# Hints for the branch at the end of a decoder kernel, and another order of tokens in its last sums

## The chip, the cores and the metric

The kernel runs on one core of a Trainium2 chip. The metric is the device time of one execution in microseconds. Three runs of the kernel before took 683.02, 683.12 and 683.7 us; the median is 683.12.

## The reference

The reference is a decoder of two layers for 4 sequences of 256 tokens, width 256, with a layer norm after each of its six blocks. Each layer has a self-attention, a cross-attention to a context of 1,601 rows and a feed-forward block. What matters here is the last block, a mixture of eight experts of which each token takes two, and the layer norm behind it:

```python
logits = SOFTCAP * jnp.tanh((x @ w_gate) / SOFTCAP)
probs = jax.nn.softmax(logits, axis=-1)
_, idx = jax.lax.top_k(probs, TOPK)                      # two of eight experts
weights = probs * jax.nn.one_hot(idx, E).sum(-2)
for e in range(E):
    h = jax.nn.silu(x @ w1[e]) * (x @ w3[e])
    out = out + h @ w2[e] * weights[:, e:e + 1]
x = _layernorm(x + out, axis=-1)
```

## The kernel before, in words

Five engines run queues of instructions, each in order: TensorE (PE), VectorE (DVE), ScalarE (ACT), GpSimd (POOL) and SyncE (SP), which issues most transfers. The program doesn't write these queues by hand. Every operation is entered into a list with its inputs, outputs and a planned cost, and `weave` (L319) then places them one by one. It takes the operation that can start first (key at L344: planned start, then priority) and appends it to its engine's queue. An operation can start when its inputs' planned ends, with a latency between the engines, have come and its engine is free. A VectorE operation of n elements is planned to be ready after `us` and to free its engine a little earlier (L244 and L245), an operation with no engine (`None`) starts at the latest planned end of what it depends on:

```python
us = 0.155 + n * (0.00055 if method == "tensor_scalar" and chip else 0.00105)
...
return us - 0.085, us
```

The planned times only fix the order. On the chip, semaphores decide when an instruction starts.

The experts' work is done in tiles of 128 rows. A tile holds tokens of one expert. `route` writes each token's row twice into a list in DRAM (`lists`), with the gate's weight and a number, its slot, behind the 256 values. The slots come from `places` (L1263 to L1266). `expert_tile` (L1439) reads 128 rows of a list (xg), multiplies them with w1 and w3 of the tile's expert (pa, in two banks of PSUM), makes h out of them (ScalarE's tanh, then two VectorE operations; tile name eh), multiplies h with w2, and makes y (tile name ey) on VectorE. VectorE then makes the row numbers (tile name slots, two small operations, L1509 to L1514), and GpSimd scatters y into rows of a DRAM tensor `yd` (L1515, issued at L1293). Each token has two rows in yd, one for each of its experts.

As many tiles as are surely needed are 20; three more exist (RARE) for an unlucky split of the tokens. The last two of the 20 tiles (`last`) don't scatter: they make a matrix `pick` of zeros and ones out of their slots (L1503 to L1508), and `add_up` (L1517) multiplies y with it, so that TensorE adds each row to its token's place in PSUM (`acc`, one bank for each of the four batches of 256 tokens). I count tiles from 1: tile 18 is the last that scatters, tiles 19 and 20 are added up. TensorE does the first products of tiles 18 and 19 one behind the other, then the w2 product of 18, the first products of tile 20, the w2 products of 19 and 20, and then the sums into acc.

SyncE reads yd back with eight transfers (L1693), two for each batch (tile name entry), which wait for all scatters. Partition p gets rows 2p and 2p+1 of its batch, which lie beside each other.

What follows stands in a branch with two arms (`end`, L1571; the switch at L1588). A number `enough` is 1 when the three rare tiles aren't needed. `ask` (L1562) lets each of the five engines read it into a register, once pick of tile 19 has been made. At the switch each engine jumps for itself into arm 0, which does the rare tiles and then `leave`, or arm 1, which does `leave` alone. Here arm 1 is taken. At an arm's start each engine runs a BRANCH_PREFETCH_HINT for the branch at the arm's end, which the switch puts there by itself.

`leave` (L1522) finishes the layer norm. GpSimd adds the two halves that were read from yd (L1541), four sums in a row. VectorE adds acc of batch b, then makes the mean and variance of batch b - 1 (L1543 to L1551), GpSimd makes rstd out of the variance in two operations (L1553, L1554), and `go` (L1526) makes nmr on VectorE, lets ScalarE scale the batch (for the last batch VectorE does one half) and issues the output's transfer. In VectorE's queue the order is: sum of batch 0, sum 1, statistics 0, sum 2, statistics 1, nmr 0, sum 3, statistics 2, nmr 1, statistics 3, nmr 2, nmr 3. In GpSimd's queue the four sums come first and the rstd pairs behind them.

Of the kernel, the functions around the change:

## Time and profile before

One execution was profiled. Its time was 681.36 us, its span from the first to the last instruction 679.6 us.

| what | value |
|---|---|
| profiled execution, us | 681.36 |
| its span, us | 679.6 |
| median of three runs, us | 683.12 |
| PE busy, us (share) | 650.4 (96%) |
| DVE busy, us (share) | 445.1 (65%) |
| ACT busy, us (share) | 305.9 (45%) |
| POOL busy, us (share) | 126.3 (19%) |
| granted TensorE clock | 0.993 |
| transfers | 85.37 MB, mean 126 GB/s |
| last TensorE sum ends, us | 668.0 |
| last output transfer issued, us | 675.34 |

PE, DVE, ACT, POOL and SP are the five engines; a q behind the name (DVEq) is the engine's sequencer, which runs branches, register and semaphore instructions. All matrix products stand at L271 and all other operations at L408, since two helpers issue them; they are told apart by the names of their tiles. In a timeline each line has the start and the length in us, engine, line, operation, tiles (out<-in) and, in brackets, how long the engine was idle before it and what released it. In the chain of waits each line is a stretch of the path that ended last. The semaphores' times and the packets of the transfers, with those of the instruction queues that bring the engines' code, are in the trace beside it.

### The profile page before, as it was taken

How to read it: one execution, taken by the hardware profiler on the slowest of the kernel's cores; microseconds unless marked ns; L12 is line 12 of the kernel's file. 1: busy time of each engine (PE TensorE's matmuls, PEld its weight loads, DVE VectorE, ACT ScalarE, POOL GpSimd, SP SyncE). 2: the span in 40 equal slices, each digit the busy share in tenths (PEclk: the TensorE clock that was granted, in tenths of full speed). 3: DMA queues.
4: the chain of work that ended last, by engine and by line, in shares of the span. 5: the costliest groups of instructions: out<-in, count | busy, mean ns of one | idle time of the engine just before them, and what ended most of it. 6: DMA issues, size and time to landing. Idle time of an engine off the chain costs nothing.

```text
span 679.6 us, 12351 instructions
## 1 busy us (share of the span) xinstructions
PE 650.4 (96%) x4373; PEld 517.3 (76%) x4373; DVE 445.1 (65%) x1196; ACT 305.9 (45%) x948; POOL 126.3 (19%) x169
## 2 busy tenths in 40 slices
PE   9999999999999999999989999999999899999993
PEld 6778788668877677786767767777866689999992
DVE  6899887433525844456499997867778665545433
ACT  4779766211132333334346786746645522222212
POOL 3331132122300000000022001131211321211114
PEclk9999999999999999999999999999999899999998
DMA  9932121536999614000020060000020282897423
GB/s 305 351 120 64 36 75 41 160 91 233 319 302 342 215 62 132 0 1 1 0 56 1 23 227 1 1 24 9 17 87 1 85 305 101 271 341 248 158 87 132
DMA packets 61456, 85.37 MB, mean 126 GB/s; under 512 B 4478, under 2 KB 43780, under 8 KB 61380
## 3 DMA queue, kind: packets, MB, share of 16 engines
q1 hardware_dynamic: 59604, 79.83, 36.2%
q0 software_dynamic: 1632, 4.48, 1.8%
q8 instruction: 39, 0.64, 0.4%
q14 instruction: 37, 0.30, 0.1%
q10 hardware_dynamic: 144, 0.13, 0.1%
HBM read 67.29 MB, written 17.13 MB: 124 GB/s over the span
## 4 chain that ended last, share of the span: by engine, by line
PE 79%; DVE 13%; ACT 4%; issue 2%; POOL 1%; DVEq 0%; POOLq 0%; ACTq 0%
PE bank L271 70%; PE bank L278 9%; ACT at L408 3%; DVE at L408 3%; DVE nm L408 2%; DVE x L408 1%; DVE as L408 1%; DVE h L408 1%; DVE st L408 1%; POOL rstd L408 1%; DVE entry L408 1%; DVE fm L408 0%; DVE hq L408 0%; DVE kf L408 0%; ACT fm L408 0%
## 5 line engine op out<-in xcount | busy, mean ns | idle before, releaser
L408 ACT ACTIVATE at<-at,nm 128x128 f32<-128x128 f32 (+1 forms) x256 | 106.3, 419 | 23.4 <-DVE nm L408 22.6
L271 PEld LDWEIGHTS bank<-xgT,wt 128*128 128x128 f32 x640 | 73.3, 192 | 1.5 <-ACT xgT L408 1.0
L271 PE MATMUL bank<-xgT,wt 128*128 128x128 f32 x640 | 73.9, 275 | 0.5 <-ACT xgT L408 0.5
L278 PE MATMUL bank<-ident,at 128*128 128x128 f32 (+1 forms) x440 | 61.6, 277 | 2.0 <-DVE at L408 1.8
L278 PEld LDWEIGHTS bank<-ident,at 128*128 128x128 f32 (+1 forms) x440 | 50.6, 142 | 14.3 <-issue 6.6
L271 PE MATMUL bank<-V,aT 128*128 128x256 f32 (+1 forms) x240 | 55.1, 380 | 0.6 <-DVE o L408 0.6
L271 PE MATMUL bank<-KT,qT 128*128 128x512 f32 (+1 forms) x128 | 54.7, 554 | 0.0
L271 PEld LDWEIGHTS bank<-V,aT 128*128 128x128 f32 (+1 forms) x240 | 45.2, 190 | 10.6 <-issue 3.6
L271 PE MATMUL bank<-kf,V 128*128 128x256 f32 (+1 forms) x208 | 50.0, 382 | 1.1 <-DVE kf L408 1.1
L408 POOL TENSOR_SCALAR rstd<-mv 128x2 f32<-128x2 f32 (+1 forms) x26 | 5.8, 223 | 242.9 <-DVE mv L408 179.2
L408 DVE TENSOR_REDUCE nm<-at 128x4 f32<-128x512 f32 (+1 forms) x64 | 50.6, 807 | 0.4
L271 PE MATMUL bank<-wkv,KT 128*128 128x256 f32 (+1 forms) x208 | 49.6, 382 | 0.0
L408 ACT ACTIVATION_READ_ACCUMULATOR at<-at,nm 128x1 f32 x256 | 48.5, 189 | 0.0
L271 PEld LDWEIGHTS bank<-kf,V 128*128 128x128 f32 (+1 forms) x208 | 38.5, 190 | 7.3 <-DVE kf L408 2.3
L271 PEld LDWEIGHTS bank<-wkv,KT 128*128 128x128 f32 (+1 forms) x208 | 37.9, 186 | 7.0 <-issue 1.0
L408 ACT COPY aT<-bank 128x512 f32<-128x512 f32 (+2 forms) x58 | 30.7, 554 | 26.5 <-PE bank L278 25.8
L408 DVE TENSOR_REDUCE m<-bank 128x1 f32<-128x512 f32 (+1 forms) x32 | 20.4, 639 | 29.7 <-PE bank L271 29.7
L408 POOL TENSOR_TENSOR at<-at,rs 128x512 f32<-128x512 f32 (+1 forms) x20 | 22.9, 1143 | 87.6 <-DVE rs L408 80.4
L408 DVE TENSOR_TENSOR at<-at,rs 128x512 f32<-128x512 f32 (+1 forms) x44 | 38.4, 872 | 0.9
L408 ACT ACTIVATE fm<-bank 128x512 f32<-128x512 f32 (+2 forms) x33 | 17.9, 551 | 45.6 <-PE bank L271 45.0
L271 PE MATMUL bank<-w2e,eh 128*128 x160 | 37.7, 380 | 0.0
L408 DVE TENSOR_TENSOR at<-bank,cmask 128x256 f32<-128x256 f32 (+1 forms) x64 | 33.2, 545 | 5.3 <-PE bank L271 5.1
(267 smaller groups left out, 1230.0 us busy)
## 6 DMA issues: line engine op xcount, KB each, us to landing
wt<-in_w SPq DMA_DIRECT2D x40, 512.0 KB, 5.2
lists<-h SPq DMA_DIRECT2D x6, 1548.0 KB, 19.2
KT<-in_ctxT SPq DMA_DIRECT2D x6, 1024.0 KB, 6.1
V<-in_ctx SPq DMA_DIRECT2D x6, 1024.0 KB, 6.4
w2e<-in_w SPq DMA_DIRECT2D x8, 512.0 KB, 7.5
KT<-in_ctxT SPq DMA_DIRECT2D x6, 577.0 KB, 6.0
V<-in_ctx SPq DMA_DIRECT2D x6, 512.0 KB, 4.2
xg<-lists SPq DMA_DIRECT2D x20, 129.0 KB, 4.1
```

Of the source, the lines that this page charges most:

```text
L271: lambda: self.nc.tensor.matmul(real(o), real(lhsT), real(rhs), start=real(start), stop=stop, **kw)
L278: fns.append(lambda: self.nc.tensor.transpose(real(o), real(x), real(ident)))
L408: return getattr(engine, method)(*[real(x) for x in args], **{k: real(x) for k, x in kw.items()})
```

## The change

`ask` becomes `tell`, which is called twice. It reads `enough` into a register on the engines that it is given, then gives these engines a hint for the switch (`tc.switch_hint`), which computes the address of the arm that will be taken and hands it to the engine's instruction prefetch. VectorE, GpSimd, SyncE and ScalarE read and hint when h of tile 19 is planned to be done; TensorE when y of tile 19 is. `expert_tile` returns h as well for that.

The slots in `places` are no longer 2p + t for the token of partition p and half t but p + 128 t, so a token's row in yd is the token's own number. Reading yd back is unchanged and now gives partition p the tokens 2p and 2p + 1, and the output is written in that order: 2 KB in a row from each partition for batches 0 to 2. `iotaT` and so `pick` are unchanged.

```diff
         places = pool.tile((P, B, 2, 2), F32, "places")
         k.gpsimd.iota(
-            places, [[S, B], [1, 2], [T, 2]], base=1, channel_multiplier=2, allow_small_or_imprecise_dtypes=True
+            places, [[S, B], [P, 2], [T, 2]], base=1, channel_multiplier=1, allow_small_or_imprecise_dtypes=True
         )
...
-            return pick, y
+            return pick, y, h
...
-    def add_up(b, into, pick, y, first=False):
+    def add_up(b, into, pick, y, _, first=False):
...
-            to = out[b * S : (b + 1) * S, :].rearrange("(t p) d -> p t d", p=P)
+            to = out[b * S : (b + 1) * S, :].rearrange("(p t) d -> p t d", p=P)
...
-    def ask(enough, picked):
-
-        engines = (nc.tensor, nc.vector, nc.gpsimd, nc.sync, nc.scalar)
+    def tell(enough, what, *engines):
 
         def emit():
-            where.update({e.engine: e.value_load(enough.real()[0:1, 0:1], min_val=0, max_val=1) for e in engines})
-
-        k.op({None: (0.0, 0.1, emit)}, [], [enough, picked], unordered=True)
+            mine = {e.engine: e.value_load(enough.real()[0:1, 0:1], min_val=0, max_val=1) for e in engines}
+            tc.switch_hint(mine, 2, "end")
+            where.update(mine)
+
+        k.op({None: (0.0, 0.1, emit)}, [], [enough, what], unordered=True)
...
-            for arm in tc.Switch(where, 2):
+            for arm in tc.Switch(where, 2, "end"):
...
         if last == 0:
-            ask(enough, two[0])
+            tell(enough, two[2], nc.vector, nc.gpsimd, nc.sync, nc.scalar)
+            tell(enough, two[1], nc.tensor)
```

## The prediction, made before the result

> **What bounds the kernel now.** I first read the page's row of busy engines: PE is busy for 96% of the span, so only the last stretch, where PE has nothing left, can be shortened by this change. Then the chain of waits from 655 us on. Its columns are start, length, work.

> ```profile
> 654.96 6.15 PE bank L271 x40
> ...
> 661.38 0.06 DVEq L1769
> 661.44 5.55 issue
> 667.00 0.06 DVEq L1588
> ...
> 667.20 0.06 DVE entry L408
> ...
> 670.83 0.04 DVE nmr L408
> 670.87 0.60 DVE entry L408
> ...
> 673.49 0.17 DVE nmr L408
> ```

> VectorE's branch (L1769) ends at 661.44, and the first instruction of its arm, the hint at L1588, starts 5.55 us later. "issue" means that no recorded work explains it. The packet records of the instruction queue do: two 8 KB packets start at 665.04, one for VectorE and one for SyncE, 3.6 us after VectorE's branch, because the reads of yd hold the 16 DMA engines from 658.85 to 665.65. GpSimd and ScalarE branched before those reads and needed only 2.6 and 2.4 us. So the arm's code arrives late, and the additions (entry) begin at 667.20.

> Next, what else those additions need: the timeline of GpSimd, and SyncE's waits.

> ```profile
> 655.12 0.96 POOL L1293 DMA_INDIRECT yd<-ey,slots  x1 [7.91 <-DVE slots L408]
> 661.78 1.27 POOL L408 TENSOR_TENSOR entry<-entry 128x512 f32<-128x512 f32 x1 [5.69 <-DMA entry<-yd]
> 663.58 3.99 POOL L408 TENSOR_TENSOR entry<-entry 128x512 f32<-128x512 f32 x3 [0.54 <-DMA entry<-yd]
> 669.45 0.23 POOL L408 TENSOR_SCALAR rstd<-mv 128x2 f32<-128x2 f32 x1 [1.89 <-DVE mv L408]
> 669.77 0.72 POOL L408 TENSOR_TENSOR rstd<-rstd,mhalf 128x2 f32<-128x2 f32 x1
> ```

> ```profile
> SPq L285 <- DMA yd<-ey,slots: 20.1, 1, 20.1
> ```

> The last scatter goes out at 655.12, lands at 657.71 (its semaphore), and only then does SyncE issue the eight reads of yd. GpSimd's four sums of what they bring end at 667.57, and its rstd work comes behind them. This second chain is covered by 5.55 us of missing code today.

> Last, the group of L1567, the reading of `enough`, as VectorE pays for it now (min/median/max ns, first and last start):

> ```profile
> L1567 DVEq EVENT_SEMAPHORE  x5: 49/50/50, 616.8 to 617.2; - x5
> ...
> L1567 DVEq TENSOR_LOAD <-enough x1: 543/543/543, 617.7 to 617.7; - x1
> L1567 DVEq FUSED_REGOPS  x1: 222/222/222, 618.3 to 618.3; - x1
> L1567 DVEq SEQ_ASSERT  x1: 31/31/31, 618.5 to 618.5; - x1
> ```

> From the first of these at 616.82 to the next vector operation at 618.61 VectorE's queue stands still for 1.79 us. The five waits are for events long past, since this is the first time that VectorE's sequencer reads; they go wherever the read goes.

> **The change, part by part.**

> *The hint itself (a gain at VectorE).* What does a hinted branch cost? Each arm starts with a hint for the branch at its end: VectorE's second branch, at 674.49, is 75 ns long and the next instruction starts at 675.07, behind a 0.41 us operation; SyncE's ends at 676.07, next 676.47. So 0.4 us, against 5.55. PE gives the counter-example: hint at 667.62, branch at 668.34, and that branch lasts 4.18 us, so a hint needs some 2.5 us (what GpSimd and ScalarE waited for a load with idle DMA). VectorE's new hint should come at about 656.0, its branch at 661.4: 5 us. [...] by the rows it starts its arm at 661.8. I take the rows. [...]

> *Where the read and hint land.* The planner, from which I take an order and no time, gives `tell` the end of h of tile 19 as its start. It counts VectorE free 0.085 us before a result ends (L245), so ey of tile 18, which is ready by then, is placed first, and slots of tile 18, which needs ey, after. VectorE's queue becomes: eh of 19, ey of 18, **read and hint**, slots of 18, eh of 20. Behind the read stand the two slots operations, and for them waits the last scatter; for it the eight reads of yd; for those GpSimd's four sums.

> *Its price there.* ey of 18 runs from 654.10 to 654.59; today slots follows at 654.50. In the trace the next operation came 1.05 us after the end of the operation ahead of the read (617.56 to 618.61). The hint adds two MOVE, a FUSED_REGOPS and the hint: 0.24 us from the rows ahead of VectorE's branch (661.14 to 661.38) and 0.11 for the hint with its gap (667.00 to 667.10). So slots starts at 654.59 + 1.05 + 0.35 = 655.99, **1.5 us later**. Bounds: 0.9 if the read need not wait for the operation before it and the old waits vanish; 2.0 if the read is slower or an assertion is added. The row is exact for this read, so 1.5. eh of 20 (656.51) is still untouched by it.

> *What that does downstream.* Scatter 656.62, landing 659.21, reads from 659.26. The DMA engines are saturated by them (2 MB in 6.8 us), so everything shifts: GpSimd's last sum ends at 667.57 + 1.50 = 669.07. Only then rstd of batch 0: 0.06 gap, 0.31 to the start of pow (669.45 to 669.77), 0.73 to its event (669.77 to 670.50), so 670.18, and nmr of batch 0 on VectorE at 670.24 instead of 670.74. VectorE itself is no longer late: its additions wait for GpSimd's sums at 664.5, 666.4, 667.8 and it has the statistics of batch 1 done by 669.5. But the addition of batch 3 stands behind nmr of batch 0 on VectorE's queue, so it starts at 670.29 instead of 670.79. PE's sums end at 668.01 and are not last. From that addition on the order and lengths are those of today: **0.50 us gained** to the end. In general the gain is 2.0 minus the delay of slots: with no delay nmr would start at 668.74.

> *The other engines' reads and hints: nothing.* ScalarE: between the activation at 650.59 and own at 654.67, some 4 us for about 1.6; without the cover eh of 20 would slip. GpSimd: between scatters that end at 647.2 and start at 655.12. SyncE: before its 20 us wait, ahead of the eight reads, all done long before they may go. TensorE: after the second products of tile 20 and before the sums into acc. Its read took 0.70 (617.07 to 617.77), hint 0.38: 1.08. The sequencer has issued tile 20's last products by about 658.85, and the sums' first operand (ey of 19) is announced at 659.90, their first weight load starts at 660.71: hidden, at worst 0.3, and 1.1 without that cover. What is taken away at 579 (GpSimd) to 618 was hidden under PE, which had no gap there: no gain. Earlier arms on GpSimd, ScalarE and SyncE gain nothing either: they then wait for data (661.78, 670.96, 672.07).

> *The order of tokens.* The iota of places has as many elements. Scatters still write 1 KB rows. The last outputs of batches 0 to 2 go out as 128 pieces of 2 KB instead of 256 of 1 KB: a 1 KB packet took 48 ns in the outputs, a 2 KB packet 94 ns in the reads of yd, so 0.77 and 0.75 us on 16 engines: nothing. Batch 3's halves keep 1 KB pieces, with a stride of 2 KB in DRAM, which no row here shows; bounds 0.3 either way for the tail, value 0.

> *Sum.* Profiled execution 681.36 (span 679.6 and 1.76 around it) minus 0.50 is 680.86. The median of the runs is 1.76 above that execution; carried over, 683.12 - 0.5 = **682.6**.

> **Rivals.**
> - *The read costs VectorE little* (faster). If slots were delayed by no more than 0.6 us, the gain is 1.4 or more; with no delay 683.12 - 2.0 = 681.1. For it: VectorE idles 1.04 us just ahead of ey of 18, where a read would be nearly free. Against: the planned order puts it behind ey. 18%.
> - *The hint doesn't carry to VectorE's branch* (slower; place: 661.44). Its block is not kept or never fetched. Then the fetch queues behind the reads of yd as before, and these now end 1.5 us later: the packet starts at 666.5, the arm at 668.5, and everything after it 1.5 us later than today: 684.6. It decides as soon as the block is missing at 661.44 while the reads run. [...] Against: the packets of the instruction queue (25 of 8 KB from 22 to 655 us for 3,118 recorded instructions of four engines) make a line about 125 instructions, of which VectorE runs 12 between hint and branch, and its last crossing fits the 0.4 us gap at 617.3, 70 instructions before. 14%.
> - *The likeliest*, one wait replaced by another, 0.1 to 1.1 us gained: 682.0 to 683.0. 68%.

> **How the numbers follow.** A measurement of this kernel tells 0.2% (1.4 us) from no change. So faster 0.18, same 0.68, slower 0.14 are the three cases. The range reaches from the faster rival's 681.1 to 684.2, which leaves out the worst of the slower one and the tails, together under 2 in 10; the likeliest alone has 682.0 to 683.0.

> **What would show it.** Right: no "issue" of microseconds behind VectorE's branch; slots of 18 near 656.0 and the last scatter near 656.6; GpSimd's sums ending near 669.1 and nmr of batch 0 waiting for rstd near 670.2; PE's sums ending at 668.0 as before. Wrong: slots still at 654.5 (then about 681.1); a gap of more than 1 us between VectorE's branch and its arm (then about 684.6); or a gap on PE ahead of the sums at 660.9.

## The result, and the profile after

The kernel after takes 683.68 us (median of 20 runs), the kernel before in the same comparison 682.25 (20 runs): a ratio of 1.0023, 95% interval 1.0012 to 1.0033. It is slower by 1.4 us, where I had forecast 0.5 us less. The profiled execution of after took 684.53 us, its span is 682.8.

The two profiled executions differ by 3.2 us, twice what the medians do. TensorE's last sum ends at 670.23 us instead of 668.00, and up to there nearly every instruction of the experts' stage comes 2.2 us later. Of this 1.91 us is there when VectorE makes `enough` (581.36 us instead of 579.45), ahead of everything that hints and reads can touch: it is the spread of executions, in which the last sum lies between 666.40 and 670.36 over all 16 profiled kernels of this study. The other 0.32 us comes behind it. From `enough` to the last sum it is 88.87 us in the kernel after, 88.84 in e4 and 88.54 or 88.55 in all others, e6 below among them, which reads the number at the same places. So below I count from TensorE's last sum wherever two kernels are compared.

These are lines of the kernel after for reading the number (L1565), the hint (L1566), the branch (L1770) and the beginning of an arm (L1588), those of VectorE and SyncE. The columns are engine and operation, number, min/median/max ns, first and last start. The first start of L1770's COMPARE_BRANCH is the branch in question, the second is the one at the arm's end:

```profile
L1565 DVEq TENSOR_LOAD <-enough x1: 542/542/542, 656.8 to 656.8; - x1
...
L1566 DVEq BRANCH_PREFETCH_HINT  x1: 68/68/68, 658.2 to 658.2; - x1
...
L1770 SPq COMPARE_BRANCH  x2: 37/52/67, 666.5 to 679.5; - x2
...
L1770 DVEq COMPARE_BRANCH  x2: 63/73/83, 663.6 to 678.0; - x2
...
L1588 SPq BRANCH_PREFETCH_HINT  x1: 36/36/36, 667.0 to 667.0; - x1
...
L1588 DVEq BRANCH_PREFETCH_HINT  x1: 45/45/45, 669.3 to 669.3; - x1
```

VectorE is given its hint at 658.2, branches at 663.6 and starts its arm at 669.3: 5.65 us, as long as without a hint (5.55). Its instruction packet starts only at 666.77, 3.2 us behind the branch. SyncE, hinted at 584.1, needs 0.46 us from branch to arm instead of 4.98. Of the other engines (not shown) TensorE profits (0.4 us instead of 3.3), ScalarE (2.8 instead of 2.4) and GpSimd (2.65 and 2.63) don't.

GpSimd's timeline of the kernel after:

```profile
658.92 0.96 POOL L1292 DMA_INDIRECT yd<-ey,slots  x1 [9.48 <-DVE slots L408]
665.02 1.26 POOL L408 TENSOR_TENSOR entry<-entry 128x512 f32<-128x512 f32 x1 [5.13 <-DMA entry<-yd]
667.70 1.27 POOL L408 TENSOR_TENSOR entry<-entry 128x512 f32<-128x512 f32 x1 [1.42 <-DMA entry<-yd]
670.24 1.27 POOL L408 TENSOR_TENSOR entry<-entry 128x512 f32<-128x512 f32 x1 [1.28 <-DMA entry<-yd]
671.87 1.27 POOL L408 TENSOR_TENSOR entry<-entry 128x512 f32<-128x512 f32 x1 [0.36 <-DMA entry<-yd]
673.11 0.23 POOL L408 TENSOR_SCALAR rstd<-mv 128x2 f32<-128x2 f32 x1
```

Less the 2.23 us by which TensorE is late in this execution, the scatter goes out 1.57 us later than before, but the last sum starts 3.34 us later: now the third and fourth sum wait for their reads too, and the last three have 0.4 to 1.4 us of idle time ahead. And rstd follows at once, where in the kernel before GpSimd had 1.89 us to spare ahead of it. The chain of waits has turned accordingly (start, length, work):

```profile
658.92 2.55 DMA yd<-ey,slots
...
664.50 1.24 SPq L285
...
665.79 5.92 DMA entry<-yd
...
671.87 1.27 POOL entry L408
673.14 0.21 POOL rstd L408
673.35 0.07 issue
673.42 0.74 POOL rstd L408
674.16 0.02 issue
674.18 0.16 DVE nmr L408
```

VectorE's missing code, which ended last before, is no longer on it, though it is still missing. The path is scatter, reads of yd, GpSimd's sums, rstd, nmr.

One stretch of this chain is new: SyncE's seventh issue, at 664.50, takes 1.24 us, where the others take 0.34 to 0.57. SyncE's eight issues of before, of after and of e6 (below), in this order:

```profile
657.76 3.74 SPq L285 DMA_DIRECT2D entry<-yd  x8
661.53 4.68 SPq L285 DMA_DIRECT2D entry<-yd  x8
658.74 3.67 SPq L285 DMA_DIRECT2D entry<-yd  x8
```

So in the kernel after the last read goes out 0.94 us later behind the first than before. TensorE's hinted packet is under way for most of that issue (664.41 to 665.37 us). In the other kernels seven of SyncE's issues take over 0.1 us more than usual, and six of these have an instruction packet beside them; that the packet holds them up is not shown.

**A rule for the end.** nmr of batch 0 comes at the later of two times: 3.55 us after VectorE's first addition (its own queue: 667.20 to 670.74 before), or 1.04 us after the end of GpSimd's last sum (673.14 to 674.18 after). From it to the last nmr it is 3.7 to 3.8 us in every kernel. In all 16 profiles the rule gives nmr of batch 0 within 0.05 us. (The fourteen kernels e1 to e14 are the experiments below.) The table has these times, counted from the end of TensorE's last sum. "Reads" is the time from the first of SyncE's eight issues to the end of the last 2 KB packet. "PE packet" says whether a 16 KB packet of TensorE's instruction queue starts within the first 7 us of them. In the eight kernels without one a packet of TensorE, fetched behind its branch, still starts 7.1 to 8.2 us behind the first issue, ahead of the end of the reads. A dash stands where VectorE's path ends before TensorE's last sum.

| kernel | VectorE branch to arm, us | reads, us | PE packet | VectorE's path | GpSimd's path | nmr 0 | ratio to before, interval |
|---|---|---|---|---|---|---|---|
| before | 5.55 | 7.89 | no | 2.75 | 0.61 | 2.74 | 1 |
| after | 5.65 | 9.42 | yes | 2.84 | 3.95 | 3.95 | 1.0023 (1.0012 to 1.0033) |
| e1 hints earlier | 0.52 | 9.64 | yes | - | 2.14 | 2.14 | 0.9984 (0.9975 to 0.9994) |
| e2 behind a crossing | 5.85 | 9.11 | yes | 3.04 | 1.81 | 3.04 | 1.0001 (0.9989 to 1.0012) |
| e3 order alone | 4.57 | 7.90 | no | 1.76 | 0.82 | 1.76 | 0.9993 (0.9981 to 1.0004) |
| e4 after slots | 5.44 | 9.46 | yes | 2.65 | 1.69 | 2.65 | 0.9995 (0.9982 to 1.0007) |
| e5 = e1, no PE hint | 0.52 | 9.00 | no | - | 1.54 | 1.54 | 0.9981 (0.9969 to 0.9993) |
| e6 = after, no PE hint | 4.80 | 7.94 | no | 1.98 | 2.44 | 2.44 | 1.0007 (0.9996 to 1.0017) |
| e7 = e2, padded | 0.52 | 9.36 | yes | - | 2.11 | 2.11 | 0.9987 (0.9969 to 1.0005) |
| e8 PE hint alone | 5.49 | 8.68 | yes | 2.68 | 1.27 | 2.67 | 1.0001 (0.9985 to 1.0017) |
| e9 three hints | 0.52 | 8.09 | no | - | 0.69 | 0.68 | 0.9975 (0.9965 to 0.9985) |
| e10 = e9, PE late | 0.52 | 8.86 | yes | - | 1.38 | 1.38 | 0.9992 (0.9974 to 1.0009) |
| e11 = e9, PE early | 0.52 | 9.24 | no | - | 1.69 | 1.69 | 0.9980 (0.9971 to 0.9989) |
| e12 VectorE alone | 0.52 | 9.20 | no | - | 1.90 | 1.90 | 0.9987 (0.9974 to 0.9999) |
| e13 = e9, read again | 0.52 | 8.72 | no | - | 2.15 | 2.15 | 0.9983 (0.9972 to 0.9994) |
| e14 = e13, PE late | 0.52 | 9.26 | yes | - | 2.78 | 2.77 | 0.9993 (0.9984 to 1.0002) |

A line of the table is one profiled execution, its ratio is from 12 to 22 runs. For after against before the table's nmr says +1.21 us, 1.53 with the 0.32 us ahead of the last sum; the medians say +1.43.

### The profile page after: what moved, and what is told of

It is laid out like the page before. It is cut to its first block, busy times and chain, and to the rows that moved or that the text cites. A ratio compares the mean times of both kernels' runs of the same rounds, so it can differ in the third digit from the quotient of the medians.

```text
span 682.8 us, 12377 instructions
## 1 busy us (share of the span) xinstructions
PE 652.4 (96%) x4369; PEld 518.8 (76%) x4373; DVE 445.6 (65%) x1196; ACT 305.7 (45%) x948; POOL 126.0 (18%) x169
## 4 chain that ended last, share of the span: by engine, by line
PE 69%; DVE 11%; issue 11%; ACT 4%; POOL 3%; DMA 1%; SPq 1%; POOLq 0%; ACTq 0%; DVEq 0%
PE bank L271 60%; PE bank L278 9%; DVE at L408 3%; ACT at L408 3%; DVE nm L408 2%; POOL yd L1292 2%; DVE x L408 1%; DMA entry<-yd 1%; POOL rstd L408 1%; SPq L285 1%; DVE h L408 0%; DVE fm L408 0%; DVE as L408 0%; DMA yd<-ey,slots 0%; DVE st L408 0%
## 5 line engine op out<-in xcount | busy, mean ns | idle before, releaser
L408 ACT ACTIVATE at<-at,nm 128x128 f32<-128x128 f32 (+1 forms) x256 | 106.6, 421 | 22.6 <-DVE nm L408 21.8
L271 PEld LDWEIGHTS bank<-xgT,wt 128*128 128x128 f32 x640 | 73.3, 192 | 1.5 <-ACT xgT L408 1.0
L271 PE MATMUL bank<-xgT,wt 128*128 128x128 f32 x640 | 73.9, 275 | 0.5 <-ACT xgT L408 0.5
L278 PEld LDWEIGHTS bank<-ident,at 128*128 128x128 f32 (+1 forms) x440 | 51.1, 143 | 14.2 <-issue 6.8
L271 PE MATMUL bank<-V,aT 128*128 128x256 f32 (+1 forms) x240 | 55.1, 380 | 0.6 <-DVE o L408 0.6
L271 PE MATMUL bank<-KT,qT 128*128 128x512 f32 (+1 forms) x128 | 54.7, 553 | 0.0
L271 PEld LDWEIGHTS bank<-V,aT 128*128 128x128 f32 (+1 forms) x240 | 45.2, 190 | 10.6 <-issue 3.6
L271 PE MATMUL bank<-kf,V 128*128 128x256 f32 (+1 forms) x208 | 50.0, 382 | 1.1 <-DVE kf L408 1.1
L408 DVE TENSOR_REDUCE nm<-at 128x4 f32<-128x512 f32 (+1 forms) x64 | 50.6, 809 | 0.4
L408 POOL TENSOR_SCALAR rstd<-mv 128x2 f32<-128x2 f32 (+1 forms) x26 | 5.8, 223 | 241.2 <-DVE mv L408 177.2
L271 PE MATMUL bank<-wkv,KT 128*128 128x256 f32 (+1 forms) x208 | 49.6, 382 | 0.0
L408 ACT ACTIVATION_READ_ACCUMULATOR at<-at,nm 128x1 f32 x256 | 49.1, 192 | 0.0
L271 PEld LDWEIGHTS bank<-kf,V 128*128 128x128 f32 (+1 forms) x208 | 38.5, 190 | 7.3 <-DVE kf L408 2.3
L271 PEld LDWEIGHTS bank<-wkv,KT 128*128 128x128 f32 (+1 forms) x208 | 37.9, 186 | 7.0 <-issue 1.0
L408 ACT COPY aT<-bank 128x512 f32<-128x512 f32 (+2 forms) x58 | 30.7, 555 | 26.5 <-PE bank L278 25.7
L408 DVE TENSOR_REDUCE m<-bank 128x1 f32<-128x512 f32 (+1 forms) x32 | 20.5, 640 | 29.7 <-PE bank L271 29.7
L408 POOL TENSOR_TENSOR at<-at,rs 128x512 f32<-128x512 f32 (+1 forms) x20 | 22.8, 1142 | 88.3 <-DVE rs L408 81.1
L408 DVE TENSOR_TENSOR at<-at,rs 128x512 f32<-128x512 f32 (+1 forms) x44 | 38.4, 872 | 0.9
L408 ACT ACTIVATE fm<-bank 128x512 f32<-128x512 f32 (+2 forms) x33 | 17.9, 553 | 46.3 <-PE bank L271 45.7
L271 PE MATMUL bank<-w2e,eh 128*128 x160 | 37.7, 380 | 0.0
L408 DVE TENSOR_TENSOR at<-bank,cmask 128x256 f32<-128x256 f32 (+1 forms) x64 | 33.3, 546 | 5.3 <-PE bank L271 5.1
```

What stands on the lines that cost most here:

```text
L271: lambda: self.nc.tensor.matmul(real(o), real(lhsT), real(rhs), start=real(start), stop=stop, **kw)
L278: fns.append(lambda: self.nc.tensor.transpose(real(o), real(x), real(ident)))
L408: return getattr(engine, method)(*[real(x) for x in args], **{k: real(x) for k, x in kw.items()})
```

## The experiments

**Theories.** After the result I held this. *Crossing theory:* the code of VectorE, ScalarE, SyncE and GpSimd comes in lines, one to a packet of 8 KB (all 42 long packets of their queue in after have that size; about 125 instructions each by the prediction's estimate). A hint counts if it runs before its engine enters the line that holds the branch; one that runs later is lost. Rivals: the hint has no effect on some engines (dead hint), or it only needs to come early enough (lead time). For the time: tile 18's slots, delayed by the read, and the longer reads of yd. For the reads I had two theories, the new order of tokens and TensorE's hinted instruction packet.

Packets of the instruction queue name no engine. After 600 us and ahead of the first branch each kernel has three, one each for VectorE, ScalarE and SyncE; which is whose I took from the count of recorded instructions, and e7 settles it for VectorE.

### e1: the hints ahead of the last crossing

```diff
-            tell(enough, two[2], nc.vector, nc.gpsimd, nc.sync, nc.scalar)
...
+        if i == 3:
+            tell(enough, two[2], nc.vector, nc.gpsimd, nc.sync, nc.scalar)
```

> The kernel after, with the read and hint of VectorE, ScalarE, SyncE and GpSimd asked for when h of tile 11 is planned to be done instead of h of tile 19: VectorE's hint then lies at about 613 us, ahead of the instruction packet near 626 us that I take for VectorE's last crossing into a new line of code, and tile 18's slots have nothing ahead of them. Crossing theory (a hint counts on VectorE and ScalarE if it runs before the engine enters the line that holds the branch): VectorE's branch to its arm 0.4 to 0.6 us instead of 5.6, ScalarE's too instead of 2.8, no instruction packet in between; slots of 18 as in the kernel before, so if the eight reads of yd take 6.8 us again, nmr of batch 0 comes 2.0 us earlier than in the kernel before: ratio to it 0.997 (682.3 to 680.3 us); if the reads take 8.4 us as in the kernel after, GpSimd's sums end 1.6 us later and the gain is 0.4 us, ratio 0.9995. Dead-hint theory (these engines take no notice of this hint wherever it lies): stall 5.5 us as before, ratio 1.000. Lead-time theory (the hint only has to come early enough, 5.4 us was too little): as the crossing theory here.

VectorE's lines of e1 (hint L1567, branch L1772, arm L1589):

```profile
L1567 DVEq BRANCH_PREFETCH_HINT  x1: 63/63/63, 613.0 to 613.0; - x1
...
L1772 DVEq COMPARE_BRANCH  x2: 63/73/83, 662.8 to 675.3; - x2
...
L1589 DVEq BRANCH_PREFETCH_HINT  x1: 45/45/45, 663.4 to 663.4; - x1
```

0.52 us from branch to arm, ScalarE 0.41. The dead-hint theory falls. The kernel is faster than before, 0.9984 (0.9975 to 0.9994), and by less than the 2.0 us of VectorE's arm, since the reads took 9.64 us and GpSimd's path ends last.

### e2: the hints behind it

```diff
-        if i == 3:
+        if i == 7:
```

> As e1_before_crossing, but asked for when h of tile 15 is planned to be done: VectorE's hint at about 636 us, 10 us behind the packet that I take for VectorE's last crossing and some 27 us ahead of its branch; ScalarE's hint at about 634 us, ahead of ScalarE's last packet (641.7 us). Crossing theory: VectorE stalls 5.5 us at its branch as in the kernel before, ScalarE starts its arm 0.4 to 0.6 us after its branch; slots of 18 not delayed, so the time is that of the kernel before, ratio 1.000 (up to 1.001 if the reads of yd take 8.4 us). Lead-time theory: both engines 0.4 us, ratio 0.997 as in e1. Dead-hint theory: VectorE 5.5 us, ScalarE 2.5 us, ratio 1.000.

The groups of e2 for VectorE, and the hints of ScalarE and SyncE:

```profile
L1567 ACTq BRANCH_PREFETCH_HINT  x1: 65/65/65, 632.2 to 632.2; - x1
L1567 DVEq BRANCH_PREFETCH_HINT  x1: 63/63/63, 634.0 to 634.0; - x1
L1567 SPq BRANCH_PREFETCH_HINT  x1: 45/45/45, 634.1 to 634.1; - x1
...
L1772 DVEq COMPARE_BRANCH  x2: 63/73/83, 661.3 to 674.7; - x2
...
L1589 DVEq BRANCH_PREFETCH_HINT  x1: 45/45/45, 667.2 to 667.2; - x1
```

VectorE had 27 us and lost its hint: 5.85 us. SyncE, which started its arm in 0.46 us with a hint at 584 or 611, lost the one of 634.1: 5.65 us. ScalarE went against my expectation (2.49 us instead of 0.5), and speaks for the theory all the same: here its crossing's packet starts at 631.75 and not at 641, so its hint came 0.5 us too late. I had the packet's time from the kernel after, where ScalarE's queue does not have the read's instructions ahead of the crossing. GpSimd is the case against mere lead time: hinted at 580 to 583 in seven kernels, behind a crossing near 561, it branches some 75 us later and needs 2.5 to 2.7 us each time.

### e7: the same hint, another line

This is e2 with 77 writes to a small tile, which nothing uses, in VectorE's queue hundreds of microseconds earlier. VectorE's code has 74 instructions more ahead of the hint, and from hint to branch there are the same 37. I had put the last crossing of e2 some 76 instructions ahead of the branch. With about 125 to a line, 74 more should move the crossing behind it to some 25 ahead of the branch (76 + 74 - 125, an estimate), between hint and branch.

```diff
         l0_cross(b)
+        if b == 1:
...
+            pad = tiny((P, 1), "pad")
+            for _ in range(77):
+                k.vector.memset(pad, 0.0)
```

> e2_behind_crossing with 77 writes to a 128x1 tile added on VectorE in layer 0's cross-attention, hundreds of us ahead, which the result does not use (74 instructions more in VectorE's code in all); VectorE's queue from there to the branch is otherwise unchanged, with the hint 37 instructions and some 27 us ahead of the branch as in e2. [...] Crossing theory: the hint is now honoured, VectorE starts its arm 0.4 to 0.6 us after its branch instead of 5.9, and a packet near 645 us shows the crossing. Lead-time, distance and dead-hint theories: 5.5 to 5.9 us as in e2, since none of these changes. ScalarE and SyncE as in e2 (2.5 and 5.6 us). Time: that of e1 if the hint works (0.9984), of e2 if not (1.000), in either case plus what the 4.6 us of padding cost in a stretch in which VectorE is busy for less than half: up to 2 us, so the time does not decide.

VectorE's lines of e7 (branch L1778):

```profile
L1567 DVEq BRANCH_PREFETCH_HINT  x1: 63/63/63, 634.5 to 634.5; - x1
...
L1778 DVEq COMPARE_BRANCH  x2: 63/73/83, 661.7 to 674.3; - x2
...
L1589 DVEq BRANCH_PREFETCH_HINT  x1: 45/45/45, 662.3 to 662.3; - x1
```

0.52 us instead of 5.85, with the hint's place, its distance and its lead time unchanged. Of e2's packets at 620.2, 624.5 and 631.8 the first is gone, and a new one starts at 642.5 (645 was expected): it is VectorE's crossing, moved from ahead of the hint to behind it. I count the crossing theory as shown for VectorE, and as agreeing with every case on ScalarE, SyncE and GpSimd. SyncE (4.28 us) and ScalarE (2.69) lose their hints here as in e2.

### e4: VectorE's read behind slots

```diff
-            tell(enough, two[2], nc.vector, nc.gpsimd, nc.sync, nc.scalar)
-            tell(enough, two[1], nc.tensor)
+            tell(enough, two[2], nc.gpsimd, nc.sync, nc.scalar)
+            tell(enough, two[1], nc.vector, nc.tensor)
```

> The kernel after, with VectorE's read and hint asked for together with TensorE's, when y of tile 19 is planned to be done: on VectorE's queue they then stand behind slots of tile 18, eh of 20 and ey of 19, ahead of ey of 20. So the last scatter is not delayed. If the delay of slots made the kernel after slower: slots near 654.5 us (plus what the execution drifts), scatter and reads as before, GpSimd's sums end as before, nmr of batch 0 as before, ratio 1.000 (up to 1.0005, since ey of 20 comes up to 0.3 us later). If something else of the change did (the longer reads by the new order, or SyncE's and GpSimd's reads at 581 us): ratio 1.002. VectorE's stall at its branch 5.5 us by the crossing theory and by the dead-hint theory, and also by lead time (hint 1 us ahead of the branch).

The ratio is 0.9995 (0.9982 to 1.0007); its interval does not meet that of after. VectorE's hint is lost as in after (5.44 us), TensorE's packet is in the reads as in after (9.46 us). What is gone is the delay: slots stand 13.78 us ahead of TensorE's last sum (13.50 before, 11.94 after). So the delay is necessary for the loss. It may not be the whole of it: e6, which has the same delay, lost less.

### e3 and e8: the order alone, TensorE's hint alone

e3 is the kernel before with the new order of tokens and no hints:

```diff
-            places, [[S, B], [1, 2], [T, 2]], base=1, channel_multiplier=2, allow_small_or_imprecise_dtypes=True
+            places, [[S, B], [P, 2], [T, 2]], base=1, channel_multiplier=1, allow_small_or_imprecise_dtypes=True
...
-            to = out[b * S : (b + 1) * S, :].rearrange("(t p) d -> p t d", p=P)
+            to = out[b * S : (b + 1) * S, :].rearrange("(p t) d -> p t d", p=P)
```

e8 is the kernel before with TensorE's late read and hint and no other hint. Against the kernel after, apart from the old order:

```diff
-            tell(enough, two[2], nc.vector, nc.gpsimd, nc.sync, nc.scalar)
+            tell(enough, two[0], nc.vector, nc.gpsimd, nc.sync, nc.scalar, hint=False)
             tell(enough, two[1], nc.tensor)
```

> The kernel before with the new order of tokens alone (places and the outputs' pattern), no hints. Two theories on why the eight reads of yd took 8.4 us instead of 6.8 in the kernel after. Order theory: rows scattered in the new order are read back slower: 8.4 us here too; GpSimd's sums then end near 669.3 us instead of 667.6, still covered by VectorE's missing code: nmr of batch 0 at 670.5 instead of 670.7, ratio 1.000. Chance or collision theory: 6.8 us as before, ratio 1.000. The times cannot tell them apart, the packets can. My prediction gave the order nothing, bounds 0.3 us either way: ratio 0.9995 to 1.0005.

> The kernel before (old order of tokens, the four other engines read where they did and get no hint), with TensorE's late read and hint alone. Packet theory: TensorE's 16 KB packet starts 3 to 6 us behind the reads' first issue, the last 1 to 1.5 us of the reads run on one DMA engine, GpSimd's last sum starts 10 us behind the first issue instead of 8.5 and ends near 669.1 us in the times of the kernel before; VectorE's missing code covers that: nmr of batch 0 between 670.5 and 671, ratio 1.000, at most 1.0005. Other causes: 8.5 us as in the kernel before, ratio 1.000.

The order is not what lengthens the reads: 7.90 us in e3. The ratio 0.9993 (0.9981 to 1.0004) leaves its worth within my bounds or a little better. With TensorE's hint alone the reads take 8.68 us, with a TensorE packet 5.2 us into them; GpSimd's last sum starts 9.3 us behind the first issue (10 was expected, 8.5 before). As expected, none of it reaches the end while VectorE's code is missing: nmr stays at 2.67, ratio 1.0001 (0.9985 to 1.0017).

### e6 and e5: without TensorE's hint

```diff
-            tc.switch_hint(mine, 2, "end")
+            if hint:
+                tc.switch_hint(mine, 2, "end")
...
-            tell(enough, two[1], nc.tensor)
+            tell(enough, two[1], nc.tensor, hint=False)
```

> The kernel after without TensorE's hint, so that only the delay of tile 18's slots by 1.5 us is left of the two things that I hold to have lengthened GpSimd's path. Packet theory: first issue of the reads to the start of GpSimd's last sum 8.6 us instead of 10.3; GpSimd's sums end 1.5 us later than in the kernel before (669.1 in its times), rstd of batch 0 would allow nmr at 670.2; VectorE's code is still missing for about 5.6 us, so its additions begin near 667.2 to 668.5 and nmr of batch 0 comes at 670.7 to 672: ratio to the kernel before 1.000 to 1.002. Otherwise, if the hint of TensorE has no part in it: as the kernel after, nmr 1.2 us later, ratio 1.002.

> e1_before_crossing without TensorE's hint (TensorE still reads the number). In the traces of the kernels with TensorE's hint (after, e1, e2, e4) a 16 KB instruction packet of TensorE's queue starts 2.9 to 6.3 us behind the first of the eight reads' issues, and the reads' last 1.0 to 1.5 us have one single 2 KB packet under way at a time; in the kernel before and in e3 that packet starts at 7.5 us, when the reads are nearly done. Packet theory: TensorE's hint fetches its arm in the middle of the reads and holds one of the 16 DMA engines for 1 us, so the reads' last piece comes 1.5 us late. Then here: the packet behind the reads, TensorE's branch 3.3 us long again (nothing waits for it), GpSimd's sums end as early as in the kernel before (first issue to start of the last sum 8.6 us instead of 10.1 to 10.3), VectorE's arm in time, nmr of batch 0 2.0 us earlier than in the kernel before: ratio 0.997. If the longer reads come from something else (SyncE's hint, VectorE's early arm): as e1, ratio 0.9984.

e6 behaves as expected: no packet by TensorE's hint in the reads (the one behind its branch starts at 7.10 us), 7.94 us, nmr at 2.44 and a ratio of 1.0007 (0.9996 to 1.0017), against after's 1.0023. The delay of slots is still in it. e5 does not: the reads took 9.00 us although TensorE's packet came late, at 7.64 us, with two single packets of 1.05 and 1.13 us in the middle (on the mean a packet of the reads takes some 94 ns), and the ratio, 0.9981 (0.9969 to 0.9993), is hardly better than e1's. So a packet fetched by TensorE's hint is not the only thing that lengthens the reads.

### e9 to e12: which hints are worth it

e9 is e5 without GpSimd's useless hint:

```diff
-            tell(enough, two[2], nc.vector, nc.gpsimd, nc.sync, nc.scalar)
+            tell(enough, two[2], nc.gpsimd, hint=False)
+            tell(enough, two[2], nc.vector, nc.sync, nc.scalar)
```

e10 adds TensorE's late hint to it:

```diff
-            tell(enough, two[1], nc.tensor, hint=False)
+            tell(enough, two[1], nc.tensor)
```

e11 has TensorE's read and hint ahead of TensorE's last crossing instead:

```diff
+        if i == 9:
+            tell(enough, two[1], nc.tensor)
```

e12 has the old order of tokens and VectorE's hint alone:

```diff
-            tell(enough, two[2], nc.gpsimd, hint=False)
-            tell(enough, two[2], nc.vector, nc.sync, nc.scalar)
+            tell(enough, two[2], nc.gpsimd, nc.sync, nc.scalar, hint=False)
+            tell(enough, two[2], nc.vector)
```

> e5_no_pe_hint without GpSimd's hint too (GpSimd and TensorE still read the number): hints for VectorE, ScalarE and SyncE alone, when h of tile 11 is planned. Packet theory: no packet of TensorE inside the reads of yd, which end 7.9 us behind their first issue as in before, e3 and e6 (in e5 they took 9.0, with two single packets of over 1 us, which I take for chance); GpSimd's last sum starts 8.6 us behind the first issue, nmr of batch 0 comes 2.0 us earlier: ratio to the kernel before 0.997. If the 9.0 us of e5 was no chance but belongs to the arms that come early: 9.0 again and ratio 0.998.

> e9_three_hints with TensorE's late hint added, where the kernel after has it. Packet theory: a 16 KB packet of TensorE 3 to 6.5 us behind the first issue, reads end 8.7 to 9.6 us behind it, GpSimd's last sum 0.7 to 1.6 us later than in e9 and everything behind it too: ratio 0.9985, and in any case slower than e9 on the same chip. If TensorE's packet costs nothing: the same as e9.

> e9_three_hints with TensorE's read and hint asked for when y of tile 17 is planned: in TensorE's queue they then lie between the first products of tiles 18 and 19, near 650 us, and have no idle time over them. Packet theory: TensorE's arm is fetched before the reads begin (packet near 653 us), the reads end 7.9 us behind their first issue as in e9, TensorE's branch takes 0.4 us. The read costs TensorE's queue between 0 (if its products are issued far enough ahead) and 1.1 us, and the scatter of 18 as much: ratio 0.997 to 0.9985. If TensorE drops a hint given ahead of its last line, as VectorE does behind it: branch 3.3 us, packet near 665 us, otherwise the same time.

> The old order of tokens and one single hint, VectorE's, when h of tile 11 is planned; the other engines read the number and get no hint. If VectorE's late arm is the only thing that the hints can mend: VectorE 0.5 us from branch to arm, ScalarE 2.5, SyncE 4.5 to 5, TensorE 3.3 as in the kernel before, none of which anything waits for; reads end 7.9 us behind their first issue, nmr of batch 0 2.0 us earlier: ratio 0.997, as e9. If SyncE's or ScalarE's arm or the new order has a part in the gain: nearer to 1.000 than e9.

e9 has the lowest ratio of the study: 680.71 against 682.58 us, 0.9975 (0.9965 to 0.9985), though its interval meets those of most of the others. GpSimd's timeline of e9, and behind it that of e10:

```profile
655.72 0.96 POOL L1292 DMA_INDIRECT yd<-ey,slots  x1 [7.91 <-DVE slots L408]
661.90 1.26 POOL L408 TENSOR_TENSOR entry<-entry 128x512 f32<-128x512 f32 x1 [5.22 <-DMA entry<-yd]
664.28 3.95 POOL L408 TENSOR_TENSOR entry<-entry 128x512 f32<-128x512 f32 x3 [1.12 <-DMA entry<-yd]
668.19 0.24 POOL L408 TENSOR_SCALAR rstd<-mv 128x2 f32<-128x2 f32 x1
```

```profile
654.99 0.96 POOL L1292 DMA_INDIRECT yd<-ey,slots  x1 [7.91 <-DVE slots L408]
661.04 1.26 POOL L408 TENSOR_TENSOR entry<-entry 128x512 f32<-128x512 f32 x1 [5.08 <-DMA entry<-yd]
663.63 1.27 POOL L408 TENSOR_TENSOR entry<-entry 128x512 f32<-128x512 f32 x1 [1.33 <-DMA entry<-yd]
665.60 2.61 POOL L408 TENSOR_TENSOR entry<-entry 128x512 f32<-128x512 f32 x2 [0.70 <-DMA entry<-yd]
```

In e9 the last sum ends 12.5 us behind the scatter's start (668.24 less 655.72), in e10 13.2, in after 14.2. The transfers of the first 7.2 us of the reads, summed by queue, of e9 and then of e10 (queue and kind, packets, MB, share of the DMA engines):

```profile
q1 hardware_dynamic: 1099, 2.02, 81.3%
q14 instruction: 1, 0.01, 0.4%
```

```profile
q1 hardware_dynamic: 991, 1.82, 75.9%
q8 instruction: 1, 0.02, 0.9%
q14 instruction: 1, 0.01, 0.5%
```

q8 is TensorE's instruction queue. Its one packet of 1.0 us takes 0.9% of the engines' time in that stretch, but 5.4% is missing to the others, 108 packets. Most of that was lost earlier: at 5.43 us, when TensorE's packet starts, e10 is already behind e9 by 72 of the 101 packets of 2 KB that it lacks at 7.2 us. SyncE's third issue had taken 0.69 us instead of 0.37, beside another instruction packet. So this pair of profiles does not show that TensorE's packet is what lengthened e10's reads.

In after, e1 and e4 the reads' last microsecond has a single packet under way at a time, in after from 8.6 to 9.42 us behind the first issue. I read this as one DMA engine left behind, the one that carried TensorE's code, but the records name no engine. In e1 the times fit: TensorE's packet ends 7.289 us behind the first issue, four packets of the reads follow that each start 14 or 15 ns ahead of the end of the one before (at 7.275, 7.491, 7.704 and 7.922 us), and with the fourth of these begins the tail, packet behind packet to the reads' end. e5 and e12 have such a tail without a hint for TensorE. There the packet behind its branch runs beside it (7.64 to 8.59 and 7.51 to 8.88 us), and four of the last packets of the reads take 0.22 to 0.29 us each instead of the usual 0.084.

e11's TensorE took its early hint: its branch lasts 0.36 us and no packet of it starts in the first 8 us of the reads (one does at 8.21). Those took 9.24 us all the same, and the ratio, 0.9980 (0.9971 to 0.9989), is within the range expected. e12's VectorE needs 0.52 us with no other hint given, and 0.9987 (0.9974 to 0.9999) is an improvement; in its profile the reads took 9.20 us without a TensorE packet in the first 7, with four packets of 0.73 to 0.81 us. Whether the other hints or the order of tokens have a part in e9's gain these intervals do not tell.

### e13 and e14: the read added where nothing covers it

```diff
         if last == 0:
+            tell(enough, two[2], nc.vector, hint=False)
```

> e9_three_hints with a second reading of the number on VectorE, without a hint, at the place where the kernel after has it (between ey and slots of tile 18). VectorE's arm is in time, so GpSimd's sums are what ends last and nothing covers a delay. Slots of 18 come 0.9 to 1.1 us later than in e9 (the read without the hint's five instructions), and with them the scatter, the reads, GpSimd's sums, nmr of batch 0 and the end: ratio to the kernel before 0.999, 0.0015 above e9's 0.9975. If the delay had nothing to do with the time: 0.9975.

> e13_read_again with TensorE's late hint: both costs of the kernel after, but VectorE's hint honoured. Packet theory: reads end 8.7 to 9.6 us behind their first issue instead of 7.9 to 8.1 (up to 9.2 by chance), and the ratio is 0.001 to 0.0015 above e13's, some 1.0005. If TensorE's packet costs nothing: as e13, 0.999.

e13 missed its purpose. A second read of the number on VectorE has no five waits ahead of it and starts 0.01 us behind ey's start, beside ey: slots come only 0.30 us later, not 0.9 to 1.1. Its ratio, 0.9983 (0.9972 to 0.9994), can't tell 0.3 us from nothing. e14 is e13 with TensorE's late hint, as e10 is to e9. Against e13, on one chip, it gives the cost of that hint once more: reads 9.26 instead of 8.72 us, ratio 0.9993 (0.9984 to 1.0002), 0.0010 above e13's.

**TensorE's hint, all together.** Without a packet of TensorE in their first 7 us the reads took 7.89 to 9.24 us, mean 8.50 of eight profiles; with one 8.68 to 9.64, mean 9.22 of eight. In the four pairs that differ by TensorE's late hint alone the ratio with it is higher by 0.0016 (after, e6), 0.0003 (e1, e5), 0.0017 (e10, e9) and 0.0010 (e14, e13). Each pair's intervals overlap, and only the last two pairs ran side by side on one chip, but all four have one sign, and their mean, 0.0012 or 0.8 us, is near the 0.7 us of the reads. So the hint costs about 0.8 us where GpSimd's path ends last. That its packet does this by holding a DMA engine is my reading and not shown. Without the hint the reads still vary by 1.3 us. The packet behind TensorE's branch may be a part of that, since in e5, e12 and e13 it lies beside slow packets of the reads; no run keeps it out of the reads, and the cause stays open.

## Why the prediction was wrong, point by point

- **The bound, right.** VectorE's missing code ended last, and behind it lay GpSimd's path with 2.0 us to spare. The table's line of before shows both (2.75 and 0.61, so 2.1).
- **"I take the rows": the first step that failed.** I gave VectorE 0.4 us from branch to arm, since hints that had 5 us seemed to work; it was 5.65. My rows, the hints at the arms' starts, need not be of the same kind: there the hint stands in code that has just been fetched (in before two packets start at 665.04, and this hint of VectorE at 667.00). No run tests whether that is the difference. I even had VectorE's last crossing ahead of the hint and argued from it that the hint would carry. e7 shows that it is the very reason why the hint was lost: 0.52 us from branch to arm where e2 has 5.85. SyncE in after (0.46 us) and VectorE in e1, e7 and e9 (0.52) show that these two engines do take such hints. By the table this step alone takes the forecast gain away: VectorE's path ends at 2.84 us, where it ended at 2.75 before. It does not make the kernel slower, since GpSimd's path ends later still.
- **The delay of slots, right.** 1.5 us were forecast, for the planner's order that I had worked out. Slots came 3.79 us later, 1.56 without the execution's 2.23; the scatter 1.57. The hint took 0.51 us instead of 0.35, with two instructions more than I had counted, and the read ended 0.96 us behind ey instead of 1.05.
- **"so everything shifts": the second step that failed, and the one that made the loss.** I let the eight reads move by 1.50 us with their length unchanged, GpSimd's last sum ending at 669.07. It ended at 673.14, 670.91 without the 2.23, so by 3.34 instead of 1.50 us later. Most of the missing 1.84 us is the reads' length, 9.42 us instead of 7.89. In this execution 0.94 of these 1.53 us is there when SyncE sends the last read, behind its issue of 1.24 us. By the pairs above about 0.8 us goes with TensorE's hint; whether both figures are one and the same no run tells, and the rest is within what the reads vary by for a cause that I don't know. I had costed TensorE's hint as instructions on its queue ("hidden") and not as a transfer that it starts, though its fetch was bound for the stretch that I had called saturated (the DMA engines were busy for 91% of 658.85 to 665.65 in before).
- **"the gain is 2.0 minus the delay", right as a sum.** With 3.34 for the delay it gives 1.34 us lost, and 1.20 with the 2.14 us of the table (2.75 less 0.61) for the 2.0; nmr came 1.21 later, the medians say 1.43 (0.8 to 2.3). It held although VectorE's arm was late, because GpSimd's path, at 3.95, had passed VectorE's, at 2.84.
- **The other engines, right but for 0.3 us, wrong in place for SyncE.** I put SyncE's read just before its wait for the scatters; it ran at 581.5, ahead of the fetches for the late tiles, and took 2.6 us with its hint. VectorE's operations of the next tiles came up to 2 us later for that, and all but 0.3 us of that was gone by 593 us. These 0.3 us stayed to the last sum, in after and e4 but not in e6.
- **The order of tokens, right:** no measurable cost (e3).
- **The rivals.** The slower one named what happened at 661.44, a hint that doesn't carry to VectorE's branch, but not how it would cost time. It had VectorE's packet wait behind the reads and everything 1.5 us later. The packet came 5.2 us behind the first issue of the reads instead of 7.3 before, so VectorE's arm was not delayed further, and the loss came by GpSimd's sums. The faster one needed a read that costs VectorE little. It was not to be had at that place, but it is some 45 us earlier: in e9 slots stand 13.50 us ahead of TensorE's last sum, as before.

## What to carry to other kernels

A branch hint was only as good as its place in the code: given at 613 us VectorE's counted (0.52 us from branch to arm in e1), given at 634 it was lost (5.85 in e2) unless the crossing came behind it (0.52 in e7). So try it earlier, and check the gap between branch and arm in the profile: the hint's own record, 63 ns, is the same in e1 and in e2. Cost a hint as a transfer too: TensorE's, fetched beside the reads of yd, cost an estimated 0.8 us. Before an engine is given a new wait or read, find what is queued behind it: here the read stood ahead of two operations of 0.15 us that the last scatter waited for and made them 1.56 us later, and moving it (e4) or doing it earlier (e9, which also drops the hints of TensorE and GpSimd) turned 1.0023 into 0.9995 and 0.9975.
